# A four-layer network in one kernel: ends of layers 0 and 1 woven into the next stage's products, and two smaller moves in layer 2

## The chip, the cores and the metric

The kernel runs on one core of a Trainium2 chip. The metric is the time of one execution on the device, in microseconds (us); lower is better. Several runs are made and their median is taken. The engines of the core are called PE (TensorE, matrix products and transposes), DVE (VectorE), ACT (ScalarE), POOL (GpSimd) and SP (SyncE, which here does nothing but issue DMAs).

## The reference, cut to what matters

Four layers, each an attention-like part and a feed-forward part (FFN), run one after the other on x of shape 2 x 1024 x 1024 in float32. After each part there is a residual sum and a layer norm. What matters for the change:

```python
x = _layernorm(x + _L0_attn_ref(x, ...))
x = _layernorm(x + _L0_ffn_ref(x, ...))        # permuted channels, 16 small MLPs
x = _layernorm(x + _L1_attn_ref(x, ...))
x = _layernorm(x + _L1_ffn_ref(x, ...))
x = _layernorm(x + _L2_attn_ref(x, ...))       # in-projection, conv, scan, out-projection
...
# _L1_attn_ref
x = conv(inputs, conv_w, width 3, 'SAME') + conv_b     # 1024 -> 768 channels
q, k, v = split(x, 3)                                  # 256 channels each
qh, kh, vh = q @ wq + bq, k @ wk + bk, v @ wv + bv     # 16 heads of 64
o = causal softmax attention in blocks of 128, @ wo + bo
return o @ proj_w + proj_b                             # 256 -> 1024
# _L1_ffn_ref
routing = softmax(xf @ gate_w.T)                       # 8 experts
in_scale, out_scale = routing @ in_channel_scale, routing @ out_channel_scale
out = xf * in_scale @ sign(weight).T * out_scale + bias
# _L2_attn_ref
x, z = split(hidden_states @ in_proj_w, 2)             # 2048 channels each
xc = silu(causal conv of width 4 of x)
ssm_p = xc @ x_proj_w.T                                # 2048 -> 96: dt, B, C of the scan
```

## The kernel before, in words

Batch 0 is taken through all layers, then batch 1 (`net_kernel`, from L1690). A batch's tokens make 8 token tiles of 128 rows. x stays on chip twice: row form `self.x` (tokens on partitions), in which residual sums and norms are done, and transposed form `self.xT` (channels on partitions), which the products read. `to_xT(tt)` (L114) makes one tile of the second from the first: 8 PE transposes (L120) into two PSUM tiles and two copies, in turn by DVE (L97) and ACT (L99). A norm has three steps: `ln_stats` (L138, on DVE), `ln_roots` (L145 and the lines behind it, small steps going from DVE to ACT and back) and `ln_scale` (DVE, L165). Only then can `to_xT` follow.

Weights and other 512 KB tiles share one pool of 8 buffers (`self.w`, 128 x 1024 floats); a load waits on SP until the buffer's last reader is done, and every later DMA issue on SP waits with it. PSUM tiles come from 8 banks (`self.ps`).

Each engine works its instructions in order. In a `manual_schedule()` block that order is the one in which the code is written; elsewhere a scheduler orders instructions by their priority and readiness, and it has settled the order when the kernel is built.

The parts that the change touches:

- **End of layer 0** (`l0`). The FFN works on channels in another order; its outputs go by an indirect DMA to memory (`yd`) and come back transposed (`back`, 8 loads), half the tokens at a time. `add_y` turns a tile of them with 8 transposes (L443), adds it to x (DVE, L131) and takes statistics. The first four tiles' additions lie among the second half's FFN blocks. For the last four (tiles 4 to 7) there is nothing left to lie among: load, add, norm and transpose follow each other, and then layer 1 begins.
- **Layer 1's convolution** (`l1_attn`). Width 3, written for pairs of neighbouring tokens as four products (j = 0 to 3) in place of six: `sums` makes sums and differences of neighbouring columns of xT (the first token half's on DVE, L546 on, kept in `qh` and `kh`; the second half's on POOL), and each of six output chunks (`co`) has 4 x 8 matmul calls (L579; 64 rows in the trace, since each is recorded in two). In batch 0, DVE also transforms each chunk's weights (L566 to L568), and the result is stored in memory (`cvd`) for later use. In chunks 0 to 3 of batch 0 the code also issues a quarter of the dequantisation of layer 2's FFN weights (`l2_dequant`: loads, DVE steps L1378 to L1381, two indirect stores on POOL). That part isn't in a manual block. `heads` follows.
- **End of layer 1's attention.** `join(1)` makes the attention's output of the second token half (256 channels), `project(tt, nh)` the residual addition of tile tt's half nh. A list (`line`) alternates projections, norms and transposes of tiles 4 to 7, with nothing else beside them.
- **Layer 1's FFN** (`l1_ffn`). `route(th)` computes the router's logits for a token half, turns them, does a softmax and turns them back (`rT`). `signs(k)` makes the sign of a weight tile on ACT. `scale_in(tt)` multiplies xT by the input scale (two PSUM tiles from 8-partition products, L856) and splits it into `hi` (ACT) and `lo` (DVE); `scale_out(tt)` makes the output scale (L868); `product(tt, nh)` is the main product, 16 matmuls. The block's order is: both routers with signs and scaling of tile 0 between, then a loop over the 8 tiles.
- **Layer 2's input projection** (`l2_attn`, `l2_in`): 16 chunks of channels per token half: a product of 8 calls (16 rows of L104), the causal convolution on ACT and DVE, silu on ACT (L990), and `l2_px`, one call of the x projection (L997), which accumulates over all chunks. What follows (norm of the result, the scan) needs the sum of all 16.
- **Join of layer 2** (`late`): statistics of the first four tiles stand ahead of `out_proj()`.

Of the kernel before, what the change touches and what calls it, by code (L numbers as in the profile page):

```python
# [27 lines left out]
class Net:  # L28
# [97 lines left out]
    def add_row(self, row, tt):  # L126
        self.nc.gpsimd.tensor_tensor(self.x[:, tt, :], self.x[:, tt, :], row, ALU.add)

# [64 lines left out]
    def l0(self, b):  # L193
# [9 lines left out]
        with self.tc.tile_pool(name=self.nm("l0a"), bufs=1) as lp, self.tc.tile_pool(name=self.nm("l0b"), bufs=2) as tp:  # L203
# [235 lines left out]
            def add_y(tt, ys):  # L439
                for g in range(2):  # L440
                    p = self.ps()
                    for j in range(4):
                        nc.tensor.transpose(  # L443
                            p[:, j * P : (j + 1) * P], ys[4 * g + j][:, (tt % 4) * P : (tt % 4 + 1) * P], self.ident
                        )
                    self.add_x(tt, g, p)
                self.ln_stats(tt)

# [16 lines left out]
            with self.tc.manual_schedule():  # L465
# [18 lines left out]
                e = line(0, lambda tt: add_y(tt, ys), (2, 3, 3, 4, 5, 6, 6, 7, 7))  # L484
                blocks(1, e)
                ys = back(1)
                self.table()
                add_y(4, ys)
                add_y(5, ys)
                self.ln_roots([4, 5])  # L490
                for tt in (4, 5):
                    add_y(tt + 2, ys)
                    self.ln_scale(tt)
                    self.to_xT(tt)

        self.ln_roots([6, 7])
        for tt in (6, 7):
            self.ln_scale(tt)
            self.to_xT(tt)
# [5 lines left out]
    def l1_attn(self, b):  # L505
        nc, i = self.nc, self.i
        row = self.row("l1_projb")
        with self.tc.tile_pool(name=self.nm("l1a"), bufs=1) as lp, self.tc.tile_pool(name=self.nm("l1s"), bufs=2) as spool:
# [5 lines left out]
            mask = lp.tile([P, P], F, name=self.nm("mask"))  # L514
# [8 lines left out]
            bv = self.row("l1_bv")  # L523
            qkv = lp.tile([P, 6, S], F, name=self.nm("qkv"))

# [32 lines left out]
            def conv(th, co):  # L558
# [17 lines left out]
                def call(j, k):  # L576
# [9 lines left out]
                    if (j, k) == (2, 4):  # L586
                        w["f"] = spool.tile([P, HALF], F, tag="cf", bufs=1, name=self.nm("cf"))
                        for n, op in enumerate((ALU.add, ALU.subtract)):
                            nc.vector.tensor_tensor(w["f"][:, 256 * n : 256 * n + 256], w["e"], w["p", 0][:, 256:], op)
# [10 lines left out]
            first = conv(0, 0)  # L600
            first[0]()
            for j in range(4):
                for g in range(2):
                    ks = slice(4 * g, 4 * g + 4)
                    sums(nc.vector, 0, ks, [(j, (qh, kh)[j // 2][:, ks, 256 * (j % 2) : 256 * (j % 2) + 256])])
            for k in range(KD):
                sums(nc.gpsimd, 1, slice(k, k + 1), [(j, moving(1, j, k).unsqueeze(1)) for j in (2, 3, 0, 1)])
            for co in range(6):
                load, calls, last = conv(0, co) if co else first
                if co:  # L610
                    load()
                for f in calls:
                    f()
                last()
                if b == 0 and co < 4:
                    self.l2_dequant(co)

            vh = lp.tile([P, 4, D], F, name=self.nm("vh"))
# [122 lines left out]
            def join(th, wt):  # L741
                o2[th] = spool.tile([P, 2, HALF], F, tag="o2", bufs=1, name=self.nm("o2"))
# [11 lines left out]
            def project(tt, nh, wt):  # L754
# [10 lines left out]
                if nh:  # L765
                    self.ln_stats(tt)
                    self.ln_roots([tt])
# [21 lines left out]
            with self.tc.manual_schedule():  # L789
# [20 lines left out]
                attend(line(0, wp), 2)  # L810
                join(1, wo)
                for f in line(1, wp):
                    f()


    def l1_ffn(self, b):
        nc, i = self.nc, self.i
        row = self.row("l1_fb")
        with self.tc.tile_pool(name=self.nm("l1f"), bufs=1) as lp, self.tc.tile_pool(name=self.nm("l1t"), bufs=2) as tp:
            gate = self.param(lp, "l1_gate", [P, KD, 8])  # L820
            ics = self.param(lp, "l1_ics", [8, D])
            ocs = self.param(lp, "l1_ocs", [8, D])
# [9 lines left out]
            def route(th):  # L832

                p = self.ps()
                self.mm(p[:8, :], [(gate[:, k, :], self.xcols(k, th * HALF, HALF)) for k in range(KD)])
                lT = tp.tile([8, HALF], F, tag="lT", name=self.nm("lT"))
                nc.scalar.copy(lT, p[:8, :])
                p = self.ps()
                for j in range(4):
                    nc.tensor.transpose(p[:, j * 8 : (j + 1) * 8], lT[:, j * P : (j + 1) * P], self.ident[:8, :8])  # L840
                rt = tp.tile([P, 4, 8], F, tag="rt", name=self.nm("rt"))
                nc.vector.tensor_copy(rt, p[:, :32].rearrange("p (t e) -> p t e", e=8))
                self.softmax_rows(rt, [P, 4, 8], "l1f")
                p = self.ps()
                for j in range(4):
                    nc.tensor.transpose(p[:8, j * P : (j + 1) * P], rt[:, j, :], self.ident)
                nc.vector.tensor_copy(rT[:, th * HALF : (th + 1) * HALF], p[:8, :])
# [37 lines left out]
            with self.tc.manual_schedule():  # L885
                route(0)
                for k in range(KD):
                    signs(k)
                    if k == KD - 1:
                        self.table()  # L890
                    if k == 3:
                        scale_in(0)
                        scale_out(0)
                route(1)
                self.add_row(row, 0)
                for n in range(NT):
# [3 lines left out]
                    product(n, 0)  # L900
                    if n + 1 < NT:
                        scale_out(n + 1)
                    if n >= 2:
                        self.to_xT(n - 2)
                    product(n, 1)
# [5 lines left out]
        self.to_xT(NT - 1)  # L911

# [886 lines left out]
```

## Time and profile before

| what | value |
|---|---|
| median of 3 runs | 5543.17 us (5542.56 to 5547.45) |
| profiled execution, its own time | 5559.85 us |
| its span | 5557.9 us |
| granted PE clock, mean over the span | 0.948 of full speed |
| busy: PE, DVE, ACT, POOL | 5115.4, 3199.0, 1936.1, 2021.7 us |
| DMA traffic | 725.28 MB, mean 130 GB/s |
| last to_xT(3) of layer 0 to first product of the convolution (batch 0; 1) | 371.5 to 412.89; 3149.2 to 3185.42 |
| end of join(1) to first product of layer 1's FFN (batch 0) | 814.1 to 871.19 |
| first product of layer 2's projection to last x projection (batch 0) | 982.17 to 1117.66 |

All places are us from the start of the profiled execution's span. The span is what the trace shows; the execution's own time is about 2 us longer, and this one was 16.7 us above the median. In a timeline row the columns are start, duration, engine, line, operation, output <- inputs, shapes, number of instructions, and in brackets the idle time of that engine just before and what ended it. PE can run at half its clock; a transpose tile of 8 rows then takes 1.94 us and not 1.07, so durations of one kind of row tell the clock.

### The profile page before, as it was taken

How to read it: one execution, taken by the hardware profiler on the slowest of the kernel's cores; microseconds unless marked ns; L12 is line 12 of the kernel's file. 1: busy time of each engine (PE TensorE's matmuls, PEld its weight loads, DVE VectorE, ACT ScalarE, POOL GpSimd, SP SyncE). 2: the span in 40 equal slices, each digit the busy share in tenths (PEclk: the TensorE clock that was granted, in tenths of full speed). 3: DMA queues.
4: the chain of work that ended last, by engine and by line, in shares of the span. 5: the costliest groups of instructions: out<-in, count | busy, mean ns of one | idle time of the engine just before them, and what ended most of it. 6: DMA issues, size and time to landing. Idle time of an engine off the chain costs nothing.

```text
span 5557.9 us, 52406 instructions
## 1 busy us (share of the span) xinstructions
PE 5115.4 (92%) x17864; PEld 2586.7 (47%) x17864; DVE 3199.0 (58%) x4410; ACT 1936.1 (35%) x3925; POOL 2021.7 (36%) x1195
## 2 busy tenths in 40 slices
PE   9869989999999999998989799799999999999989
PEld 4436746444444444453444376464444444444533
DVE  3553245249999997214345412452599899953243
ACT  2230222257766542001013312222677665410110
POOL 1021220057778884100010211200677788831010
PEclk8789998999999999999988899989999999999999
DMA  2035310267787996110110333012777889951100
GB/s 92 33 131 174 103 43 33 100 182 221 210 234 222 259 258 197 61 60 13 55 63 33 115 123 103 32 44 87 212 215 204 243 219 264 264 177 45 61 8 30
DMA packets 263134, 725.28 MB, mean 130 GB/s; under 512 B 37425, under 2 KB 54449, under 8 KB 262869
## 3 DMA queue, kind: packets, MB, share of 16 engines
q1 hardware_dynamic: 256596, 700.97, 42.4%
q0 software_dynamic: 6272, 20.98, 1.1%
q8 instruction: 142, 2.33, 0.2%
q14 instruction: 124, 1.01, 0.1%
HBM read 616.70 MB, written 103.02 MB: 129 GB/s over the span
## 4 chain that ended last, share of the span: by engine, by line
PE 70%; DVE 14%; DMA 4%; ACT 3%; issue 2%; POOL 1%; SPq 0%; DVEq 0%; POOLq 0%; ACTq 0%
PE ps L104 28%; PE ps L1232 7%; PE ps L1122 6%; PE ps L579 5%; DVE h L1129 4%; PE ps L1151 4%; PE ps L1445 4%; PE ps L1271 3%; DVE h L1140 2%; PE ps L120 2%; PE ps L1185 2%; ACT ps L1124 1%; DVE x L165 1%; DVE st L142 1%; DMA w<-xcd 1%
## 5 line engine op out<-in xcount | busy, mean ns | idle before, releaser
L1114 POOL TENSOR_TENSOR h<-h,br 128x1024 f32<-128x1024 f32 x512 | 1204.3, 2374 | 27.6 <-DMA h<-dxd 20.0
L1124 ACT ACTIVATE ps<-ps,l_Alog 128x512 f32<-128x512 f32 x1024 | 668.8, 660 | 686.0 <-PE ps L1122 671.5
L1122 PE MATMUL ps<-hi,rep 128*128 128x512 f32 x1024 | 758.8, 741 | 22.9 <-DVE h L1129 14.6
L1129 DVE TENSOR_TENSOR_SCAN h<-ps,h 128x512 f32<-128x512 f32 x512 | 606.4, 1213 | 159.9 <-ACT ps L1124 159.8
L1129 DVE TENSOR_TENSOR_SCAN h<-ps,hst,h 128x512 f32<-128x512 f32 x512 | 643.8, 1304 | 11.7 <-ACT ps L1124 11.7
L1140 DVE TENSOR_TENSOR h<-h,ps 128x1024 f32<-128x1024 f32 x512 | 621.4, 1214 | 0.0
L104 PE MATMUL ps<-w,xT 128*128 128x512 f32 (+1 forms) x1280 | 518.3, 562 | 0.0
L1232 PE MATMUL ps<-xT,w 128*128 128x512 f32 x1024 | 511.0, 602 | 0.0
L1151 PE MATMUL ps<-h,sel 128*32 128x512 f32 x2048 | 404.5, 611 | 72.6 <-DVE h L1140 72.3
L1431 POOL TENSOR_TENSOR x<-x,row 128x1024 f32<-128x1024 f32 x48 | 112.9, 2353 | 883.4 <-PE ps L120 883.4
L131 DVE TENSOR_TENSOR x<-x,ps 128x512 f32<-128x512 f32 x192 | 129.9, 687 | 522.9 <-PE ps L104 372.5
L104 PE MATMUL ps<-xT,w 128*128 128x512 f32 x960 | 425.3, 599 | 0.2 <-DMA w<-l_wqkv 0.2
L1122 PE MATMUL ps<-lo,rep 128*128 128x512 f32 x1024 | 408.5, 399 | 0.0
L104 PEld LDWEIGHTS ps<-w,xT 128*128 128x128 f32 x1280 | 247.4, 195 | 255.3 <-issue 248.1
L1122 PEld LDWEIGHTS ps<-hi,rep 128*128 128x128 f32 x1024 | 196.0, 191 | 346.4 <-issue 242.1
L120 PE MATMUL ps<-ident,x 128*128 128x128 f32 x1024 | 168.5, 322 | 182.5 <-DVE x L165 155.8
L156 ACT ACTIVATE rs<-mv 128x1 f32<-128x1 f32 (+2 forms) x94 | 19.1, 203 | 786.4 <-DVE mv L150 786.2
L104 PEld LDWEIGHTS ps<-xT,w 128*128 128x128 f32 x960 | 183.8, 192 | 233.7 <-issue 230.4
L1122 PEld LDWEIGHTS ps<-lo,rep 128*128 128x128 f32 x1024 | 196.7, 192 | 201.0 <-issue 196.4
L1080 POOL TENSOR_TENSOR e<-e,one 128x512 f32<-128x512 f32 x64 | 81.5, 1273 | 563.5 <-ACT one L1077 381.0
L1271 PE MATMUL ps<-w,w 128*128 128x512 f32 x512 | 269.3, 608 | 0.0
L1185 PE MATMUL ps<-xT,w 128*128 128x512 f32 x512 | 266.1, 605 | 2.0 <-DVE h L1129 2.0
(268 smaller groups left out, 7579.6 us busy)
## 6 DMA issues: line engine op xcount, KB each, us to landing
h<-dxd SPq DMA_DIRECT2D x512, 512.0 KB
w<-l_in SPq DMA_DIRECT2D x128, 512.0 KB
w<-l_out SPq DMA_DIRECT2D x96, 512.0 KB
w<-l_conv SPq DMA_DIRECT2D x54, 512.0 KB
w<-cvd SPq DMA_DIRECT2D x36, 512.0 KB
w<-l_fw SPq DMA_DIRECT2D x32, 512.0 KB
xcd<-xo SPq DMA_DIRECT2D x64, 256.0 KB
szd<-zo SPq DMA_DIRECT2D x64, 256.0 KB
```

What stands on the lines that cost most here:

```text
L104: self.nc.tensor.matmul(out, lhsT, rhs, start=j == 0, stop=j == n - 1)
L120: nc.tensor.transpose(p[:, j * P : (j + 1) * P], self.x[:, tt, k * P : (k + 1) * P], self.ident)
L579: nc.tensor.matmul(w["p", j // 2][:, 256 * (j % 2) : 256 * (j % 2) + 256], w["w"][j][:, k * P : (k + 1) * P], moving(th, j, k), start=k == ...
L1114: nc.gpsimd.tensor_tensor(hs[k], hs[k], norms[of(k)[0]][1].unsqueeze(1).to_broadcast([P, 2, HALF]), ALU.mult)
L1122: nc.tensor.matmul(dA[k, m], rep[:, 8 * jj + 4 * m + q, :], hl[u, c][n], start=n == 0, stop=n == 1)
L1124: nc.scalar.activation(dA[k, m], dA[k, m], AF.Exp, scale=A[:, g : g + 1])
L1129: nc.vector.tensor_tensor_scan(hs[k][:, m, :], dA.pop((k, m)), hs[k][:, m, :], hst[:, g : g + 1] if u else 0.0, ALU.mult, ALU.add)
L1140: nc.vector.tensor_tensor(hs[k], hs[k], norms[of(k)[0]][3].unsqueeze(1).to_broadcast([P, 2, HALF]), ALU.mult)
L1151: nc.tensor.matmul(py[u, c][32 * j : 32 * j + 32, :], self.sel[:, q, :], hs[k - 1 + j // 2][:, j % 2, :], start=False, stop=q == 3,)
L1185: nc.tensor.matmul(p, w["w"][:, k * P : (k + 1) * P], self.xcols(k, u0, HALF), start=k == 0, stop=k == KD - 1)
L1232: nc.tensor.matmul(p, w["w"][:, k * P : (k + 1) * P], self.xcols(k, u * HALF, HALF), start=k == 0, stop=k == KD - 1)
L1271: nc.tensor.matmul(p, y[:, cc, t * P : (t + 1) * P], wt[:, cc * HALF : (cc + 1) * HALF], start=c2 == 0 and cc == 0, stop=last,)
```

## The change

Four parts; no arithmetic of the network changes.

1. **End of layer 0.** `l0` stops after the second half's FFN blocks and hands the address of the results to `l1_attn`. There, loads of y, `add_y`, norms and transposes of tiles 4 to 7 are placed among the calls of chunks 0 and 1 of the first half's convolution, in a manual block. The sums are made j by j. Loads of y go to `vh`, a tile of layer 1 that is not yet in use; the causal mask's temporary moves to a weight buffer, and one temporary of chunk 1 to `u0`. The dequantisation goes from chunks 0 to 3 to chunks 2 to 5.
2. **End of layer 1's attention.** `l1_attn` stops after `join(1)`; projections, norms and transposes of tiles 4 to 7 go into `l1_ffn`: router 0 first, the projections among softmax, signs and scaling, norms and transposes among products 0 and 1, router 1 among products 1 and 2. Gate and channel scales are loaded before `join(1)`, the scales into two of the eight weight buffers. The roots of the four norms become one call.
3. **Layer 2's input projection.** The x projection of chunk c-1 is issued behind the product of chunk c. The first three weight tiles are loaded within layer 1's FFN.
4. **Join of layer 2.** The statistics of tiles 0 to 3 go behind the first group of products of the loop.

The diff, cut to its core:

```diff
-                blocks(1, e)
-                ys = back(1)
-                self.table()
-                add_y(4, ys)
-                add_y(5, ys)
-                self.ln_roots([4, 5])
-                for tt in (4, 5):
-                    add_y(tt + 2, ys)
-                    self.ln_scale(tt)
-                    self.to_xT(tt)
-
-        self.ln_roots([6, 7])
-        for tt in (6, 7):
-            self.ln_scale(tt)
-            self.to_xT(tt)
+                blocks(1, e)
+        return yd[1]
...
+            c0, c1 = conv(0, 0), conv(0, 1)
+            with self.tc.manual_schedule():
+                c0[0]()
+                sums0(0)
+                sums0(1)
+                c1[0]()
+                ys = [t for q in range(4) for t in (vh[:, q, :HALF], vh[:, q, HALF:])]
+                for k, t in enumerate(ys):
+                    nc.sync.dma_start(t, yd[k * P : (k + 1) * P, :])
...
+                calls(c0, 0)
+                sums0(2)
+                calls(c0, 1)
+                calls(c0, 2)
+                calls(c1, 0)
+                self.table()
+                self.add_y(4, ys)
+                self.add_y(5, ys)
+                self.ln_roots([4, 5])
+                self.ln_scale(4)
+                self.add_y(6, ys)
+                self.to_xT(4)
+                self.ln_scale(5)
+                sums0(3)
+                calls(c1, 1)
+                self.to_xT(5)
+                calls(c0, 3)
+                c0[2]()
+                c2 = conv(0, 2)
+                c2[0]()
+                self.add_y(7, ys)
+                self.ln_roots([6, 7])
+                calls(c1, 2)
+                self.ln_scale(6)
+                self.to_xT(6)
+                self.ln_scale(7)
+                calls(c1, 3)
+                self.to_xT(7)
+                c1[2]()
...
-                if b == 0 and co < 4:
-                    self.l2_dequant(co)
+                if b == 0:
+                    self.l2_dequant(co - 2)
...
+                early = [gate] + [self.w(i[name], 8)[:8, :] for name in ("l1_ics", "l1_ocs")]
                 join(1, wo)
-                for f in line(1, wp):
-                    f()
...
             with self.tc.manual_schedule():
-                route(0)
+                self.table()
+                r0, r1 = route(0), route(1)
+                r0[0]()
+                project(4, 0)
+                project(4, 1)
+                r0[1]()
+                project(5, 0)
+                r0[2]()
                 for k in range(KD):
                     signs(k)
-                    if k == KD - 1:
-                        self.table()
-                    if k == 3:
-                        scale_in(0)
-                        scale_out(0)
-                route(1)
+                project(5, 1)
+                scale_in(0)
+                scale_out(0)
+                project(6, 0)
+                project(6, 1)
+                self.table()
+                project(7, 0)
+                project(7, 1)
+                self.ln_roots([4, 5, 6, 7])
                 self.add_row(row, 0)
                 for n in range(NT):
                     if n + 1 < NT:
                         self.add_row(row, n + 1)
                         scale_in(n + 1)
-                    product(n, 0)
-                    if n + 1 < NT:
-                        scale_out(n + 1)
-                    if n >= 2:
-                        self.to_xT(n - 2)
-                    product(n, 1)
+                    for nh in range(2):
+                        tt = 4 + 2 * n + nh
+                        if tt < NT:
+                            self.ln_scale(tt)
+                        product(n, nh)
+                        if nh == 0 and n + 1 < NT:
+                            scale_out(n + 1)
+                        if tt < NT:
+                            self.to_xT(tt)
+                        if nh == 0 and n >= 2:
+                            self.to_xT(n - 2)
+                        if n == 2:
+                            r1[1 + nh]()
+                    if n == 1:
+                        r1[0]()
+                    if n == 5:
+                        w = [self.w(i["l2_in"][c]) for c in range(3)]
...
-                w = self.w(i["l2_in"][c])
+                w = ready.pop(0) if ready else self.w(i["l2_in"][c])
                 self.mm(p, [(w[:, k * P : (k + 1) * P], self.xcols(k, u0, HALF)) for k in range(KD)])
+                if c:
+                    l2_px(u, c - 1, xo.pop())
                 xp = l2_x(u, c, p)
                 l2_taps(c, p, xp)
-                l2_px(u, c, l2_silu(u, c, p))
+                xo.append(l2_silu(u, c, p))
...
             for c in range(NCH):
                 l2_in(0, c)
+            l2_px(0, NCH - 1, xo.pop())
...
+                        if nh == 0 and c2 == 0:
+                            for tt in range(4):
+                                self.ln_stats(tt)
+                            self.ln_roots(list(range(4)))
```

`r0[0]`, `r0[1]` and `r0[2]` are the three steps of `route`: logits, softmax, turning back.

## The prediction

> **What bounds the kernel now.** I read the page first, then the chain, then TensorE's timeline at each place that the diff touches.
>
> ```profile
> PE 5115.4 (92%) x17864; PEld 2586.7 (47%) x17864; DVE 3199.0 (58%) x4410; ACT 1936.1 (35%) x3925; POOL 2021.7 (36%) x1195
> ...
> PE 70%; DVE 14%; DMA 4%; ACT 3%; issue 2%; POOL 1%; SPq 0%; DVEq 0%; POOLq 0%; ACTq 0%
> ```
>
> TensorE is busy for 92% of the span and carries 70% of the chain. The change removes no product, so it can only take from the 8% that TensorE idles (442 us) and from rows at half clock. The timeline shows where both lie: at the end of layer 0 (batch 0),
>
> ```profile
> 379.10 1.03 PE L443 MATMUL ps<-ident,y 128*128 128x128 f32 x2 [7.55 <-DMA y<-yd]
> ...
> 395.82 1.94 PE L120 MATMUL ps<-ident,x 128*128 128x128 f32 x8 [6.56 <-DVE x L165]
> ...
> 403.32 1.94 PE L120 MATMUL ps<-ident,x 128*128 128x128 f32 x8 [3.99 <-DVE cb L530]
> 409.62 3.44 PE L120 MATMUL ps<-ident,x 128*128 128x128 f32 x16 [4.36 <-DVE x L165]
> 412.89 7.07 PE L579 MATMUL ps<-qh,w 128*128 128x256 f32 x32
> ...
> 447.89 9.99 PE L579 MATMUL ps<-qh,w 128*128 128x256 f32 x32 [7.21 <-DVE w L567]
> ```
>
> at the start of layer 1's FFN,
>
> ```profile
> 817.52 1.07 PE L120 MATMUL ps<-ident,x 128*128 128x128 f32 x8 [3.38 <-DVE x L165]
> 818.43 5.30 PE L104 MATMUL ps<-w,o 128*128 128x512 f32 x8
> ...
> 833.13 1.97 PE L120 MATMUL ps<-ident,x 128*128 128x128 f32 x8 [4.37 <-DVE x L165]
> ...
> 849.75 3.78 PE L856 MATMUL ps<-rT,l_ics 8*128 8x128 f32 x16 [0.77 <-DVE rT L847]
> 853.32 3.62 PE L868 MATMUL ps<-l_ocs,rT 8*128 8x512 f32 x4
> ```
>
> and at layer 2's input projection:
>
> ```profile
> 994.08 2.02 PE L997 MATMUL ps<-xo,wx 128*96 128x512 f32 x2 [4.58 <-ACT xo L990]
> 995.89 14.13 PE L104 MATMUL ps<-xT,w 128*128 128x512 f32 x28
> ...
> 1117.66 1.10 PE L997 MATMUL ps<-xo,wx 128*96 128x512 f32 x2 [3.73 <-ACT xo L990]
> ```
>
> The bracket is the idle time before a row and what ended it. Transposes of 8 blocks take 1.07 us warm and 1.94 at half clock, so each such stall is paid twice. Batch 1 shows the same rows (first products at 3185.42, L997 again after 4.58 and 3.73).
>
> **Layer 0's end in layer 1's convolution.** Moved: 32 y transposes, 4 tiles of x transposes, their adds and norms, go between the products of output chunks 0 and 1. The four halves of the input sums are split, too, so that the first products need only to_xT(3).
>
> Before, batch 1: to_xT(3) ends at T0=3149.2, products start 36.2 us later, and two chunks of about 14.1 us (8.22+6.85 the first, half cold) bring chunk 2 to T0+65.5. After: TensorE's own work is two chunks, 28.2, y transposes 32 x 0.21 = 6.7 (17 take 3.59 at 385.66), x transposes 4 x 1.07 = 4.3, so 39.2. What it still waits for I count on VectorE: the first half of the sums (4 of 8 adds, of which the first pair at 1.22 each must be done) lies in the time that to_xT(3)'s copy takes anyway; to_xT(4) comes behind three tiles' adds (0.69 each half), stats (1.28+0.21), roots (1.45) and a scale (0.8): idle 6.3; to_xT(6) 2.6 in the same way. The loads of y (2.8 us from issue to first landing) lie behind four j-blocks of products, 14 us. Sum 47.4 to 48, so **-18** (-14 to -20).
>
> Batch 0: chunk 2 starts 76.4 us after to_xT(3) (447.89-371.5), with 7.21 idle for the weight transform. After: the same 47.4, plus waits for the transformed weights. On SP's queue the y loads now stand behind chunk 1's store of transformed weights, which waits for three adds of 1.22 behind four sums; on VectorE, chunk 2's transform (3 x 1.22, waiting for its loads) stands ahead of add_y(7), and so ahead of its norm, to_xT(7) and chunk 1's end. I take +6.6: T0+54 (50 to 60), -22.4. The dequantisation, however, moves from chunks 0..3 to 2..5. A chunk then moves 4.5 MB (three weight loads, two stores, scales, packed weights, two scatters); the three chunks of before that had it ran at 245 and 293 GB/s and took 17.3 and 17.2 us; the two without it took 14.4 and 13.9. Four at 17.2 are 68.8 for 62.7: +6.1. Its first part no longer stands in layer 0's last stretch (37.1 us there against 34.3 in batch 1): -2. Together **-18** (-8 to -25).
>
> **Second half of layer 1's projection in its FFN.** Before, from 800 to 871 us TensorE is busy for 54.70 of 71 us. Moved: router 0 ahead of the projections of tiles 4 to 7, these among softmax and scaling, their norms, transposes and router 1 into products 0 to 2. Roots of 4 to 7 become one call. The products still need signs of all eight weight tiles, in ScalarE's order ahead of hi(0). Two of the eight weight buffers now hold the channel scales, so only two of the eight FFN tiles are early; six come as buffers fall free. Two of them took about 2 us each (217 GB/s at 830 to 834), the sign 0.97: signs end near 830, product (0,0) starts at about 835 for 871.19. But then it carries what stood before it: the chain of adds, statistics, roots and scales of tiles 4 to 7 is in front of router 1 and scale_in(4). I count idle times of 2.0, 5.2, 1.8, 4.1 and 4.5 us, 17.6 in all, as much as the 16.3 before. Product (3,0) then starts at 898.6 for 911.06: -12.5, all of it from rows that were cold before, if the clock stays full.
>
> Does it? The trace:
>
> ```profile
> 814.00:818.00 4.00, 0.62 (x6) 1.00 0.00 0
> ...
> 850.00:854.00 4.00, 4.00 (x17) 0.50 0.06 25
> 854.00:858.00 4.00, 4.00 (x6) 0.50 0.06 26
> ```
>
> (columns: window, TensorE busy and instructions, granted clock, DMA share, GB/s). An idle time of 3.38 us was followed by 8 matmul rows in 5.30 us for 3.43 warm: 1.9 lost. [...] 8 us fully busy with 8-partition products stayed at 0.50. [...] a cold stretch can last 5.6 us (871.19 to 876.8, 2.3 lost) or more: 3.7 each for four, 12.5-15 = +2.5. I take **-8 per batch**[...], since most of the work between the idle times is full 128-row products, as at 818.43. Ends: +3, and -25 if VectorE's chains fit better than I count.
>
> **x projection a chunk later.** Before: silu(0) needs 4.58 us past chunk 0's products, and cold rows follow. After: it has chunk 1's 6.87. From 982.17: 16 chunks x 6.87 + 14 projections x 0.86 + 0.4 cold = 1104.5 for 1112.9; the last projection waits its 3.73 as before, behind which the norm and the scan's start stand. **-8.5 per batch** (-7 to -10). Weights loaded ahead: no wait for l_in stands in the trace, so 0.
>
> **Norm statistics in the join loop.** Nothing else of VectorE or ScalarE stands between; their order is the same, so 0 (-1 to +1).
>
> **Sum.** -18-18-16-17 = -69 on a profiled 5559.85 us (span 5557.9), which is 16.7 us above the median; the stalls don't scale with that, so I take it from the median: 5543-69 = **5474 us**.
>
> **Rivals.**
> - *More* (0.15): VectorE's chains are hidden in products and the clock stays warm: FFN -25 twice, convolution -22 and -20, projection -9 twice, -110: 5433. For it: VectorE is 37% busy there (26.52 of 71). Against it: in-order queues, and idle times on it that products can't fill.
> - *Less* (0.20): batch 0's convolution bound by DMA at some 260 GB/s over five chunks (-6), the FFN given back to a cold clock (+1 twice), convolution of batch 1 -16, projection -7 twice: -34, 5509. For it: 0.88 DMA share in a chunk with dequantisation.
> - *Slower* (0.03): starved weight buffers. ScalarE's hi(0) stands behind eight signs, VectorE's lo behind hi(0), the adds of tiles 6 and 7 behind that, and TensorE behind their norms. Each us that the last FFN tile lands after 830 is lost, twice. With -53 from the rest it turns at +26 per batch, and passes +0.2% at +32: the last tile at about 870, six tiles (3 MB) at 75 GB/s. Against it: single loads at 217 to 307 GB/s there.
> - *It doesn't do it* (0.03, no change): the scheduler's order cancels it. TensorE's order in the built kernel shows the moves, so only waits could.
>
> The likeliest, mine, has 0.59 and its own range 5452 to 5494. For 8 in 10 I go halfway to both others: 5443 to 5508. A measurement tells 0.2% (11 us) from no change: faster 0.94, same 0.03, slower 0.03.
>
> **What would show it.** Right: to_xT(3) to chunk 2's start 48 and 54 us; chunks 2 to 5 of batch 0 at 17 us with DMA share near 0.9; product (0,0) some 30 us after join(1), not 66, with idle times of 4 to 5 us before tile 4's transposes and router 1; no wait before the first L997's counterpart, about 8 us less from first products to the last projection. Wrong: ScalarE waiting for l_fw between signs; granted clock 0.5 through the woven part (my FFN term goes); chunks under 15 us in batch 0 (my +6 goes); a later stage, above all the scan, that starts earlier but ends no earlier.

## The result, and the profile after

The changed kernel takes 5480.22 us in the median (4 runs, 5474.06 to 5492.16) for 5542.86 of the kernel before (5535.69 to 5547.45): ratio 0.9889, 95% interval 0.9872 to 0.9906, 62.6 us less. Run again beside other kernels it gave 0.9891 (0.9877 to 0.9905), 5482.68 us in the median. All medians here are of fast executions; of the kernel with router 1 moved, one slow execution of six (11346.77 us) is left out. The changed kernel's profiled execution took 5492.16 us, with a span of 5490.4: 67.5 less than the span of before. From the page of the changed kernel, the engines and the chain:

```profile
PE 5096.7 (93%) x17864; PEld 2579.4 (47%) x17864; DVE 3189.5 (58%) x4380; ACT 1933.2 (35%) x3913; POOL 2027.7 (37%) x1195
...
PE 69%; DVE 13%; ACT 4%; DMA 3%; issue 2%; POOL 1%; SPq 0%; DVEq 0%; ACTq 0%; POOLq 0%
```

TensorE has the same 17864 matmuls; it is busy 18.7 us less (fewer rows at half clock: the granted clock is 0.953 in the mean, for 0.948) and idle some 49 us less. Where, the stages tell. Each is the distance between two rows of TensorE's timeline, in us, before and after. The last x projection is taken at the start of its second record, since a call leaves two:

| stage | batch 0 | batch 1 |
|---|---|---|
| end of layer 0's last FFN block to first head product | 144.0, 129.5 | 125.1, 107.8 |
| first head product to end of join(1) | 294.7, 294.4 | 295.3, 293.4 |
| end of join(1) to first product of layer 2's projection | 176.8, 168.3 | 178.7, 169.7 |
| that to the last x projection | 136.0, 127.9 | 136.0, 127.9 |

Join(1) of batch 0 ends at 805.38 in the profile of before; the 814.1 in the table ahead is the end of the five projections behind it. The three touched stages give -31.8, -17.5 and -16.2: -65.5 of the -67.5. The rest lies outside them: layer 0's blocks of batch 0 ended 6.5 earlier, the way from batch 0's last x projection to the same place in batch 1 (the scan, layer 3 and layer 0 of the next batch) took 5.6 longer, and there are smaller differences.

TensorE's timeline of the changed kernel at the end of layer 0, batch 0:

```profile
391.96 1.94 PE L120 MATMUL ps<-ident,x 128*128 128x128 f32 x8 [5.63 <-DVE x L176]
...
412.93 1.97 PE L120 MATMUL ps<-ident,x 128*128 128x128 f32 x8 [5.59 <-DVE x L176]
...
420.13 7.07 PE L568 MATMUL ps<-qh,w 128*128 128x256 f32 x32
...
457.54 9.01 PE L568 MATMUL ps<-qh,w 128*128 128x256 f32 x32 [9.61 <-DVE w L556]
...
475.75 7.14 PE L568 MATMUL ps<-qh,w 128*128 128x256 f32 x32 [2.30 <-DVE w L556]
...
489.64 27.63 PE L104 MATMUL ps<-qkv,w 128*128 128x512 f32 x64
```

The waits for y are gone, two waits for the norms are left, and chunk 2 starts (420.13) 55.1 us after to_xT(3) for 76.4. The wait for transformed weights, which was longest before chunk 2 (7.21), is longest before chunk 4 now (9.61). The last row is the first head product. In batch 1:

```profile
3115.82 1.06 PE L120 MATMUL ps<-ident,x 128*128 128x128 f32 x8 [1.16 <-DVE x L176]
3118.70 7.15 PE L568 MATMUL ps<-qh,w 128*128 128x256 f32 x32 [1.81 <-issue]
...
3141.00 1.94 PE L120 MATMUL ps<-ident,x 128*128 128x128 f32 x8 [5.63 <-DVE x L176]
...
3157.67 1.85 PE L120 MATMUL ps<-ident,x 128*128 128x128 f32 x8 [1.94 <-DVE x L176]
...
3164.60 7.07 PE L568 MATMUL ps<-qh,w 128*128 128x256 f32 x32
```

From the end of to_xT(3) to chunk 2 it is 47.7 us. At the start of layer 1's FFN:

```profile
770.00 14.00 PE L104 MATMUL ps<-qh,w 128*128 128x512 f32 x32
783.93 7.04 PE L104 MATMUL ps<-xT,l_gate 128*8 128x512 f32 x16
...
798.42 0.60 PE L890 MATMUL ps<-ident,rt 128*8 128x128 f32 x4 [1.56 <-DVE rt L198]
...
813.40 0.50 PE L104 MATMUL ps<-ws,hi 128*128 128x512 f32 x1
...
822.84 1.97 PE L120 MATMUL ps<-ident,x 128*128 128x128 f32 x8 [3.60 <-DVE x L176]
...
849.33 8.73 PE L104 MATMUL ps<-xT,l_gate 128*8 128x512 f32 x16 [4.20 <-DVE xT L97]
...
877.58 3.66 PE L902 MATMUL ps<-rT,w 8*128 8x128 f32 x16 [4.52 <-DVE rT L891]
```

The first row is join(1), the row at 813.40 the first of product (0,0), 29.4 us behind it. The old chain of waits is replaced by four: router 0, transposes of tile 4, router 1 (waiting for the copy of tile 7) and scaling of tile 4 (waiting for router 1). The last two rows also show the clock: 8.73 us for logits that took 7.04 for router 0, 3.66 for a scaling that takes 2.05. And at layer 2's projection:

```profile
952.28 14.18 PE L104 MATMUL ps<-xT,w 128*128 128x512 f32 x32
966.30 1.02 PE L1065 MATMUL ps<-xo,wx 128*96 128x512 f32 x2
...
1079.26 2.02 PE L1065 MATMUL ps<-xo,wx 128*96 128x512 f32 x2 [2.87 <-ACT xo L1058]
```

Two chunks follow each other without a gap, and the first x projection waits for nothing.

### The profile page after: what moved, and what is told of

It reads as the page before. It is cut to its first block, busy times and chain, and to the rows that moved or that the text cites. A ratio compares the mean times of both kernels' runs of the same rounds, so it can differ in the third digit from the quotient of the medians.

```text
span 5490.4 us, 52346 instructions
## 1 busy us (share of the span) xinstructions
PE 5096.7 (93%) x17864; PEld 2579.4 (47%) x17864; DVE 3189.5 (58%) x4380; ACT 1933.2 (35%) x3913; POOL 2027.7 (37%) x1195
## 4 chain that ended last, share of the span: by engine, by line
PE 69%; DVE 13%; ACT 4%; DMA 3%; issue 2%; POOL 1%; SPq 0%; DVEq 0%; ACTq 0%; POOLq 0%
PE ps L104 28%; PE ps L1302 7%; PE ps L1192 6%; PE ps L568 5%; PE ps L1221 4%; DVE h L1199 4%; PE ps L1517 4%; PE ps L1341 3%; DVE h L1210 2%; PE ps L120 2%; PE ps L1255 2%; ACT ps L1194 1%; DVE x L176 1%; DVE st L153 1%; PE ps L1130 1%
## 5 line engine op out<-in xcount | busy, mean ns | idle before, releaser
L1199 DVE TENSOR_TENSOR_SCAN h<-ps,h 128x512 f32<-128x512 f32 x512 | 606.2, 1212 | 166.0 <-ACT ps L1194 109.5
L104 PEld LDWEIGHTS ps<-xT,w 128*128 128x128 f32 x960 | 182.1, 190 | 230.1 <-issue 225.1
L1302 PEld LDWEIGHTS ps<-xT,w 128*128 128x128 f32 x1024 | 188.7, 191 | 174.7 <-issue 148.7
```

Of the source, the lines that this page charges most:

```text
L104: self.nc.tensor.matmul(out, lhsT, rhs, start=j == 0, stop=j == n - 1)
L1199: nc.vector.tensor_tensor_scan(hs[k][:, m, :], dA.pop((k, m)), hs[k][:, m, :], hst[:, g : g + 1] if u else 0.0, ALU.mult, ALU.add)
L1302: nc.tensor.matmul(p, w["w"][:, k * P : (k + 1) * P], self.xcols(k, u * HALF, HALF), start=k == 0, stop=k == KD - 1)
```

## The experiments

**Each part by itself.** Four kernels, the kernel before with one part of the diff each; the second leaves out the early load of layer 2's weights, which goes with the third.

> The kernel before with part 1 alone (end of layer 0 in the convolution, dequantisation in chunks 2 to 5). By the theory that the parts add up, each by its own stage: 36 to 38 us less than before (5505 for 5543), about 21 in batch 0 and 17 in batch 1, both complete by the first head product. By the rival that the parts share stalls or that a later stage gives time back: under 30 us less, and the projections of layer 1's end start less than 17 us earlier in each batch.

> The kernel before with part 2 alone (second half of layer 1's projection in its FFN; no weights of layer 2 loaded ahead). By the theory: 16 to 20 us less than before (about 5525), 9 to 11 of it per batch, between the end of join(1) and the last product of the FFN, with four idle times of 1.5 to 4.5 us that replace the old ones. By the rival that what the trace shows there is a cold clock that comes back elsewhere: 0 to 8 us less.

> The kernel before with part 3 alone (x projection a chunk later, three weight tiles loaded ahead). By the theory: 17 us less than before (5526), 8.5 per batch, of which 4.6 is the idle time before the first x projection, some 3 the half clock behind it and 0.9 the projection that no longer stands ahead of the last chunk's end. By the rival that the scan behind it ends no earlier, since it is paced by its own engines: under 8 us less in all, with the scan of each batch longer by what was gained.

> The kernel before with part 4 alone (statistics of tiles 0 to 3 behind the first group of products in the join loop). Order and number of instructions on every engine stay the same, so by the theory 0, within 3 us of before, and the run serves as the yardstick for what two kernels of one stream of instructions differ by. By the rival that the place matters (another wait for the statistics' operands): 4 to 8 us either way, in the out-projection of layer 2.

| kernel | median, us | ratio to before | layer 0's end to heads, batch 0, 1 | FFN stage | projection stage |
|---|---|---|---|---|---|
| convolution alone | 5511.4 | 0.9943 (0.9926 to 0.9959) | 128.9, 108.0 | 178.5, 176.7 | 136.0, 135.9 |
| FFN alone | 5519.6 | 0.9956 (0.9941 to 0.9970) | 137.0, 124.2 | 166.0, 166.4 | 136.1, 136.2 |
| x projection alone | 5533.4 | 0.9973 (0.9963 to 0.9983) | 143.4, 124.5 | 176.9, 176.6 | 127.9, 127.8 |
| statistics alone | 5548.5 | 1.0004 (0.9996 to 1.0012) | 143.2, 124.4 | 177.7, 176.8 | 135.9, 136.0 |

Each part moves its own stage and leaves the others where they were within 2 us, with one exception: the FFN's part alone shortens batch 0's convolution by 7.0 (137.0 for 144.0). There TensorE waits 6.2 us for y and 7.6 for transformed weights, where the kernel before has 10.6 and 11.1. That edit also moves the mask into a weight buffer; whether that is the cause isn't shown. The medians, -35.9, -27.7 and -13.9 against the pooled runs of before (5547.28), make -77.5, more than the -62.6 of all together, but each carries some 6 to 9 us of uncertainty, and the FFN's may hold those 7.0 (its profiled execution was the fastest of eight). By stages the convolution's part gives 32.2, as in the whole; the x projection's 16.3, as in the whole; the FFN's 23.1 in its own stage, and 17.5 in the whole. Most of that last difference is the clock: with the FFN part alone, TensorE was at half clock for 23.9 us of the loop in each batch; in the changed kernel for 30.7. So the rivals, in the sizes that they were given, are refused: the convolution's part reaches its sum, and with the x projection alone the projection stage falls by the full 8.1 and 8.2 and the stages behind it show only the differences that executions of one kernel show. Whether the scan gives a few us back, that scatter would hide.

That scatter is worth a line, since it is larger than two of the parts: from the start to the end of layer 0's blocks in batch 0, the profiled executions took 351.7 to 366.7 us, and from batch 0's last x projection to the same place in batch 1 2023.5 to 2038.3, in no order that follows the edits. In the profile of before the first of these was the longest of all. My reading in the prediction that 2 us of it belong to the dequantisation isn't shown: kernels with it there have 366.7, 351.7, 357.1 and 356.9, those without it 352.5 to 360.5.

The statistics' part changes nothing within 0.12%, as the unchanged order of instructions let expect.

**The dequantisation.** Two kernels on the chunks 2 to 5 of batch 0, 69.5 us for 55.3 in batch 1.

```diff
                 last()
-                if b == 0:
-                    self.l2_dequant(co - 2)
...
             for c in range(NCH):
                 l2_in(0, c)
+                if b == 0 and c % 3 == 2 and c < 12:
+                    self.l2_dequant(c // 3)
```

> The changed kernel with the dequantisation of layer 2's FFN weights moved on, behind chunks 2, 5, 8 and 11 of layer 2's input projection in batch 0. Chunks 2 to 5 of batch 0's convolution took 69.5 us with it, against 55.3 in batch 1. If it is what stretches them, they take 55 to 57 and the time falls by 12 to 14 us against the changed kernel (about 78 against the kernel before); if the transform of the convolution's weights (loads and stores) does it, they stay above 62 and under 7 us fall. A cost in the new place would show as chunks of the input projection above 7.73 us.

Measured: 5464.3 us, 0.9852 (0.9835 to 0.9870), 83.0 us less than before. TensorE's timeline of this kernel at the place of the stall:

```profile
443.73 7.07 PE L568 MATMUL ps<-qh,w 128*128 128x256 f32 x32
450.63 7.07 PE L568 MATMUL ps<-kh,w 128*128 128x256 f32 x32
```

Chunk 4 starts as chunk 3 ends. The four chunks take 55.3 us, so all 14.2 us were the dequantisation's, and the transform of the convolution's own weights is hidden. In the new place it costs nothing that shows (128.1 us, and 128.1 in batch 1, which has none of it). The median fell by some 20 us against the changed kernel; what that has beyond the 14.2 wasn't followed.

```diff
-            for k in range(KD):
-                sums(nc.gpsimd, 1, slice(k, k + 1), ...)
             for co in range(2, 6):
...
+            for k in range(KD):
+                sums(nc.gpsimd, 1, slice(k, k + 1), ...)
```

> The changed kernel with GpSimd's sums for the second token half issued behind chunk 5 and its dequantisation, and not ahead of chunk 2. Two theories of the 69.5 us that chunks 2 to 5 take in batch 0. Mine on record: 4.5 MB per chunk at some 260 GB/s; then nothing falls but some 3 us, since the bytes are the same. The rival, from the trace after: the second store of the dequantisation stands behind 22 us of sums on GpSimd's queue, holds its weight buffer, and VectorE waits 11.7 us for it ahead of chunk 4's weight transform; then the idle time of 9.6 us before chunk 4 goes and the chunks take 56 to 62 us, 8 to 13 us less. In batch 1 nothing changes by either, unless the sums come too late for the second half.

Measured: 5481.4 us, 0.9885 (0.9870 to 0.9900): no gain. The scheduler put the sums back early (they start at 415.25), so the edit did less than it says; but the second store of dequantisation 0 is now ahead of most of them, at 421.55 for 443.17, where it starts 0.16 us behind the last of 22.2 us of sums. TensorE's wait falls from 9.61 to 6.66 and the chunks take 66.5. From VectorE's timeline of this kernel:

```profile
434.74 3.71 DVE L1450 TENSOR_SCALAR w<-w 128x1024 int32<-128x1024 int32 x1 [5.49 <-DMA w<-l_packed]
...
446.36 1.23 DVE L555 TENSOR_TENSOR w<-w,w 128x1024 f32<-128x1024 f32 x1 [4.38 <-issue]
```

VectorE now waits for the packed weights, and then 4.38 us ahead of chunk 4's transform, for which the view names no cause (the loads of its weights were issued from 439.07 on). Freeing GpSimd's queue took 3 us off the stall and no more. What of the rest is bytes and what is buffers isn't settled by these runs. Against bytes: in the changed kernel the DMA engines were busy for 0.45 of their time in the 23.5 us that contain the stall, and 0.85 only in the next 18. For buffers: in the kernel with the sums moved, SP's queue waited for them, 17.0 us in weight loads behind VectorE's dequantisation step. Dequantisation holds four of eight, and a chunk of the convolution four.

**The end of the FFN, which the change left as it was.**

```diff
-        self.to_xT(NT - 2)
-        self.ln_scale(NT - 1)
-        self.to_xT(NT - 1)
...
                 l2_in(0, c)
+                if c == 0:
+                    tail()      # the three calls above
```

> The changed kernel with the end of layer 1's FFN treated as the change treats the others: transposes of tiles 6 and 7 and the scale of tile 7 go behind the first chunk of layer 2's input projection, which reads only tiles 0 to 3. The idle time of 5.10 us before these transposes and their half clock (3.67 for 2.1) stand in both batches. By the theory that a stall is worth its idle time and the cold rows behind it, once a product can stand in it: 6.5 to 7.5 us less per batch, 13 to 15 in all against the changed kernel. By the rival that VectorE's chain of the last tile is met again by the next waiter (transposes behind chunk 0, or its taps behind the copies): under 5 in all.

Measured: 5464.3 us, 0.9859 (0.9844 to 0.9875), 82.2 less than before and so about 20 less than the changed kernel. Its timeline there:

```profile
935.94 7.03 PE L104 MATMUL ps<-xT,w 128*128 128x512 f32 x16
942.81 1.91 PE L120 MATMUL ps<-ident,x 128*128 128x128 f32 x16
944.55 7.04 PE L104 MATMUL ps<-xT,w 128*128 128x512 f32 x16
```

In the changed kernel the same transposes stood ahead of that product:

```profile
948.82 3.67 PE L120 MATMUL ps<-ident,x 128*128 128x128 f32 x16 [5.10 <-DVE x L176]
```

They take 1.91 us for 3.67, behind a product and without a wait. From the last product of the FFN to the last x projection it is 128.8 us for 136.5: 7.7 us per batch. The rest of the 20 is again the FFN loop's clock (23.9 us cold for 30.7 in both batches) and scatter.

**The clock.** The changed kernel's windows of 3.4 us in the loop (columns: window, its length, TensorE's busy time and instructions, granted clock, DMA share, GB/s):

```profile
829.80:833.20 3.40, 3.40 (x25) 1.00 0.06 27
833.20:836.60 3.40, 3.40 (x10) 0.52 0.06 27
836.60:840.00 3.40, 3.40 (x13) 0.97 0.06 25
```

TensorE never idles in these, and yet the middle one is at half clock. The window ahead of it holds the end of a tile's transposes (to 830.2), an 8-partition scaling (`scale_in`, 830.15 to 832.2) and 1.1 us of a product. But small work alone didn't do it here. The third window, cut as the clock's record has it, holds even more of it, 1.9 us of `scale_out` and 0.7 of transposes, and the one behind it stays at full clock:

```profile
837.58 1.98 PE L914 MATMUL ps<-w,rT 8*128 8x512 f32 x4
839.49 1.09 PE L120 MATMUL ps<-ident,x 128*128 128x128 f32 x8
```

```profile
836.78:840.19 3.41, 3.41 (x14) 1.00 0.06 26
840.19:843.60 3.41, 3.41 (x18) 1.00 0.04 18
```

I counted such windows (full clock, no idle time, over 1 us of 8-partition products) in layer 1's FFN, cut at the changes of the granted clock, in all traces but that of the next kernel. Of 98 that hold a whole `scale_in` (16 matmuls, at least 1.9 us), 74 were followed by half clock; of 60 with only part of one, none; of 169 with `scale_out` in its place, 4; and all 17 that hold little but the two of them. So in this loop half clock without idle time mostly followed a whole `scale_in` within one window; why that one, and why not always, stays open.

```diff
-                        scale_in(n + 1)
+                        scale_in(n + 1, (0,))
...
-                        product(n, nh)
-                        if nh == 0 and n + 1 < NT:
-                            scale_out(n + 1)
+                        product(n, nh, mid)   # second part of scale_in or scale_out after 8 of 16 matmuls
+                        if nh == 0 and n + 1 < NT:
+                            scale_out(n + 1, (0,))
```

> The changed kernel with the 8-partition scaling products of layer 1's FFN split and placed among the main products, so that no more than some 2 us of them stand together; same work, same number of instructions. The trace shows half clock for 3 to 3.5 us also where TensorE never idles, each time about 3.4 us after such products and transposes. If small products count as idle for the clock, those cold stretches go: 1.6 us each, three to five a batch, 8 to 14 us less in all. If only true idle time sets the clock, nothing changes: within 3 us. If interleaving itself costs [...], slower by 2 to 5 us.

Measured: 5483.7 us, 0.9893 (0.9878 to 0.9908): no gain, so the 8 to 14 us didn't come. What the first and the third expectation named is in the trace. Time at half clock in the loop fell from 30.7 us to 17.1 in batch 0 and 6.8 in batch 1, and none of it follows a window without idle time any more. Against it, a tile's step with the clock full throughout takes 13.27 us (3620.70 to 3633.97), where the kernel before has 12.42 (3670.39 to 3682.81): a step now has nine pieces and not five, some 0.2 us for each that was added. Over seven tiles that is 6 us, about what 12 us less at half clock give. The loop takes 129.1 and 123.6 us for 130.3 and 130.3. The profiled execution was the fastest of the four (5467.1 us, the others 5477.2 to 5492.5), so how often the clock was kept in the others isn't known.

**The rival on the slower side.**

```diff
-   self.w(i[name], 8)[:8, :]                           for name in ("l1_ics", "l1_ocs")
+   [self.w(i[name], 8)[:8, :] for _ in range(2)]       for name in ("l1_ics", "l1_ocs")
...
-   ics[:, k * P : (k + 1) * P]
+   ics[tt % 2][:, k * P : (k + 1) * P]                 # ocs in the same way
```

> The changed kernel with the channel scales held twice, in four and not two of the eight weight buffers (even tiles read the one copy, odd tiles the other; the arithmetic is the same). It prices the rival on the slower side. By that rival every us that the last FFN weight tile lands later is lost, twice: signs end near 820 for 808.2 in batch 0, so some 12 us more per batch, 20 to 25 in all. By my reading of the trace after, signs have 5 us of slack before product (0,0) needs the last one: 3 to 8 us more per batch, and 0 if the loads still come two at a time in 2 us.

Measured: 5500.1 us, 0.9913 (0.9900 to 0.9927): 12 to 20 us more than the changed kernel, by the ratios or by the medians. ScalarE in this kernel, and then in the changed one:

```profile
806.31 1.06 ACT L865 ACTIVATE ws<-w 128x1024 fp32r<-128x1024 f32 x1 [1.81 <-DMA w<-l_fw]
807.27 0.61 ACT L908 CAST hi<-xT 128x512 fp32r<-128x512 f32 x1
```

```profile
807.13 1.06 ACT L865 ACTIVATE ws<-w 128x1024 fp32r<-128x1024 f32 x1 [0.77 <-DMA w<-l_fw]
808.10 0.61 ACT L908 CAST hi<-xT 128x512 fp32r<-128x512 f32 x1
```

The last sign ends 32.5 us after join(1), for 24.2 in the changed kernel, in batch 1 6.6 later; the FFN stage takes 177.2 and 175.9 us, 8.9 and 6.2 more. So the mechanism and its price of about one for one are real, and the 5 us of slack that I expected didn't show in the sum: product (0,0) starts only 6.9 and 3.3 later, and the loop behind it is 2.0 and 2.8 longer. But even with half of the buffers held the kernel stays faster than before.

**Part 2's order mended.**

In words and not in code:

```diff
-  to_xT(4..7) behind products (0,0), (0,1), (1,0), (1,1)
+  to_xT(4) behind (0,1), to_xT(5) behind (1,0), to_xT(6) and to_xT(7) behind (1,1)
-  r1[0] behind (1,1); r1[1] behind (2,0); r1[2] behind (2,1)
+  r1[0], r1[1] behind (2,0); r1[2] in the middle of (2,1)
```

> The changed kernel with part 2's order mended where its trace still shows waits: transposes of tiles 4, 5 and 6, 7 half a product or more later, router 1's logits behind product (2,0) and its last step in the middle of product (2,1), ahead of that product's steps on VectorE. In the changed kernel the loop has 13.9 us of idle time a batch (3.6, 4.2 and 4.5 the largest) and 23.9 or 30.7 us at half clock against 19.4 before. By the theory that each wait stands behind VectorE's queue and is paid again in half clock: 9 to 12 us less per batch, 18 to 24 in all. By the rival that VectorE is simply full there and the waits come back at the next reader: under 6 in all.

Measured: 5446.3 us, 0.9828 (0.9815 to 0.9841), against 0.9891 for the changed kernel in the same set: 36.4 us less by the medians, more than either theory had. TensorE's timeline of this kernel at router 1, which waits for nothing now:

```profile
844.73 7.04 PE L104 MATMUL ps<-xT,l_gate 128*8 128x512 f32 x16
...
856.91 0.60 PE L890 MATMUL ps<-ident,rt 128*8 128x128 f32 x4
859.30 2.05 PE L902 MATMUL ps<-rT,w 8*128 8x128 f32 x16
```

Idle time in the loop: 4.9 and 1.7 us for 12.9 and 13.1; time at half clock: 17.1 and 10.2 for 30.7 in both. The FFN stage is 155.8 and 149.3, for 169.5 and 168.8. Of the 33.2 us of the two batches, 19.4 are idle time and 17.1 are half of 34.1 us at half clock; the two overlap by a little. I had counted the idle time and left out the half clock that went with it.

**All together.** Dequantisation, the FFN's end and the router, in one kernel.

> The changed kernel with three of the edits together: dequantisation in layer 2's input projection, the FFN's last transposes behind the first chunk of that projection, and router 1 moved. By the theory that stage times add up: 14 + 16 + 20 = 50 us less than the changed kernel, 113 less than before (about 5430). By the rival that two of them meet in layer 2's input projection (VectorE's and the weight buffers' share there): 35 or less, with the projection's stage above 131 us for 128.

Measured: 5422.3 us, 0.9776 (0.9764 to 0.9789), 121 us less than before and 60 less than the changed kernel: the fastest. That is more than the 50 of the first theory, since the router's part alone gave more than was put in for it; but the second theory's sign came as well. In batch 0 the projection stage, which now also holds the transposes, has 9.3 us of idle time for 2.9 in batch 1 (139.1 for 128.9). Two of its three waits stand where batch 1 has none:

```profile
944.25 1.10 PE L1069 MATMUL ps<-xo,wx 128*96 128x512 f32 x2 [3.45 <-ACT xo L1062]
...
970.68 2.02 PE L1069 MATMUL ps<-xo,wx 128*96 128x512 f32 x2 [3.00 <-ACT xo L1062]
```

The dequantisation, free there by itself, and the last tile's work do meet in that place.

## Why the prediction was right

It said 5474, in a range of 5443 to 5508, and 5480.2 was measured. (Halfway from 5494 to 5509 is 5501 and not 5508; the measured time lies inside either.) Three parts moved what they were said to move, and the fourth nothing; in two places below, the size was met in part by luck.

- **Convolution, batch 1**, -18: measured -17.3. From to_xT(3) to chunk 2 in 47.7 us for the 47.4 to 48 of the sum; idle time ahead of to_xT(4) 5.63 for 6.3, ahead of to_xT(6) 1.94 for 2.6. In the second run of the changed kernel it is -13.6 (111.5 for 107.8): the waits are the same, but the first product ran in part at half clock, 10.11 us for 7.15.
- **Convolution, batch 0**, -18: measured -14.5. To chunk 2 it took 55.1 us (54 in the sum), and chunks 2 to 5 69.5 (68.8). The sizes held, the reason for the second didn't, and that its sum fits is luck: I had every chunk bound by bytes, but chunks 2 and 3 ran at full rate (13.8 each) and one wait of 9.61 stood before chunk 4, at a DMA share of 0.45. The 17.3 us of chunk 2 before, from which I took the rate, were misread, too: its first row there is at half clock behind a wait (9.99 for 7.07). The 2 us from layer 0's stretch aren't shown.
- **FFN**, -8 per batch, an estimate between +2.5 and the -12.5 of a full clock: measured -8.5 and -9.0. Signs ended 24 us and product (0,0) came 29.4 and 30.9 us behind join(1), as worked out (25 and 30). Idle time was less than counted (1.6, 3.6, 4.2 and 4.5: 13.9 for 17.6), the clock worse than that estimate supposed: in batch 0 30.7 us at half clock in the loop for 19.4 before, against 21.6 saved ahead of it. The two misses cancel, which is luck. Full products between the waits didn't keep the clock up, though I had argued that they would, from 818.43.
- **x projection**, -8.5 per batch: measured -8.1 twice. The last wait is 2.87 and a cold row, for 3.73 and a warm one.
- **Statistics**, 0: 1.0004 (0.9996 to 1.0012).
- **Rivals.** *More* named what was left, and the last runs show that it was there for the taking: with the waits in VectorE's order removed the FFN stage falls by 20 to 30 us per batch from before, the -25 of that rival. *Less* didn't come: none of its terms was met (-14.5 and -17.3 for its -6 and -16 in the convolution, -8.5 and -9.0 for +1 in the FFN, -8.1 for -7 in the projection). *Slower* has the right mechanism and price, but the loads didn't come late enough: between the signs ScalarE waited 2.5 us for them in batch 0.

On the clock: in the changed kernel's trace the record of the granted clock begins with stretches at half clock of 17.07, 13.65, 40.96, 17.07 and 3.41 us, multiples of 3.41, and in the loop they are 3.41 or 6.83 long. What takes the clock down or brings it back isn't settled here: the windows counted above never idle, and those with a whole `scale_in` mostly lost the next one, those with as much of other small work seldom. The 8 us at half clock that the prediction shows from 850 on hold 7 us of `scale_in` and `scale_out` and then 1 us of the router's logits: work without a gap, at a granted clock of 0.50 in both windows that the prediction prints.

## What to carry to other kernels

Weaving one stage's end into the next stage's products gained idle time and cold rows here (14.5 and 17.3 us in the convolution, 8.5 and 9.0 in the FFN); but how much was decided by the order on the engine that makes the operands (36.4 us more with router 1 moved), so look for what the new place puts ahead of the step that TensorE will wait for, and move the consumer by half a product rather than to where it looks free. Work that is only parked beside a stage (here a dequantisation for later use) had a price in that stage (14.2 us, in buffers or in bytes); beside one that takes one buffer at a time it cost nothing that shows (128.1 us with it and without). And judge such edits by distances between rows of the trace: here stages repeat within 1 to 4 us, while whole executions of one kernel scatter by 5 to 35.

## What was not expected of the hardware

TensorE dropped to half clock without a gap in its work, too: in the changed kernel's loop it was at half clock for 30.7 of 130.3 us, with 13.9 us idle, and four of its nine windows at half clock in batch 0 follow one without any idle time (those at 833.37, 867.50, 908.46 and 922.11); with small products split, for 6.8 of 123.6 with 10.3 us idle in batch 1, and 17.1 of 129.1 with 11.8 in batch 0. The number of windows at half clock isn't fixed for a kernel: the loop of the changed kernel's FFN, and that of kernels with the same loop, had either 23.9 or 30.7 us, seven or nine windows, and took 126.6 to 126.9 or 128.4 to 130.3 us. What sets the one or the other wasn't tried; a guess, from the counts above (74 of 98 windows with a whole `scale_in`, none of 60 with a part), is how the stretches of 3.41 us happen to fall on the loop.
